# Masked attention on gathered rows: the first batch by its least key, counts and mask sums in the score banks, and transfers in smaller portions

## The chip, the cores and the metric

The kernel runs on one core of one Trainium2 chip. The metric is the device time of one execution in microseconds (us). Before the change the median of three runs is 963.98 us (963.57 to 964.73). The engines have short names in what follows: PE is TensorE (PEld its weight loads, which overlap the matmuls), DVE is VectorE, ACT is ScalarE, POOL is GpSimd, SP is SyncE, which here issues most DMAs. Lines such as L823 are line numbers of the kernel before, unless it is said that they are of the kernel after.

## The reference

There are 16 batches of 512 features by 1024 tokens, fp32, and one mask value (0 or 1) per token and batch. With `xt` the transposed x, per batch:

```python
q = xt @ Wq.T                                   # T x 512, used as q, k and v; 8 heads of 64
scores = scale * einsum('bhqd,bhkd->bhqk', qh, qh)
logits = (scores * cmask + (1.0 - cmask) * NEG) * rmask
attn = softmax(logits, axis=-1)
ctx = einsum('bhqk,bhkd->bhqd', attn, qh)
out = ctx @ Wo.T
return x + transpose(out)                       # residual
```

A masked key gets weight 0. A masked query has all logits 0, so its output is a mean over all tokens, the same row for every masked token of a batch. Only the active tokens (mask 1) need real attention.

## The kernel before, in words

**Only active rows.** At the start the kernel counts the active tokens of each batch with matmuls on the mask, and forms for each batch a key, 32 times the count plus the batch's number (`order`, L198 to L210). The batches are worked in the order of rising keys. For that, DVE ranks all keys against each other: a compare of 16 x 16 pairs and a sum. From then on "batch b" means the batch at place b. `permute` picks the mask of the batch at a place out of all masks, `sources` the number of that batch, from which the base of its rows in memory follows. `slots_of` (one batch, L286 to L316) and `slots` (a group of batches, L244) give each active token its slot, with a prefix count by matmuls against a triangle of ones. `hot` (L356) forms a one-hot matrix of the low part of the slots (128 x 1024 fp16, L360); `index` (L363) multiplies it with a second one-hot matrix on PE (L369) and so gets the list of row numbers (L372). With it `gather` (posted to POOL, indirect DMA, L458) brings the active rows of x from memory, in blocks of 128 rows: four blocks, and a fifth where a batch is handled at 528 or 544 columns instead of 512. At the end the rows of the output are written through the same lists (L1051).

**One batch.** The rows are transposed on PE (`xt`, L562), split into fp16 high and low parts (L520, L521), and multiplied with Wq, also split (`query`, three matmuls a part, L591). Queries are split again and spread by SP into `xx`, a layout in SBUF with both heads of a pair (`qsplit`, L606 to L628). Four pairs of heads follow: `scores` (L823) forms the scores of a pair in two steps, four score tiles each, and ACT takes their exponentials out of PSUM (L838). `attend` (L858) multiplies them with the values. The reciprocals of the sums are formed in two parts: `recip_sums` (DVE, up to L905) and `recip_rows` (L907): a transpose on PE (L912), a copy of ten rows out of PSUM (`rr`, L917), a DMA to DRAM (`rd`, L920) and two DMAs back, which spread the rows over partitions (`rb`, L924). `norm` scales the context with them and splits it (L964 to L968); `project` (L982) multiplies with Wo, and L988 adds the residual.

**PSUM.** In the steady part the tile `pss` has six of the eight banks. Scores use its banks 0 to 4 or a part of them, the context banks 4 and 5; small products ("spots") stand in the first columns of bank 5: the index lists, the score bounds (`top`, `bottom`, L714 to L730). The two banks that are left are a ring, `pm`, which queries, transposes, values, projections, the counts of `slots`, the mask sum (`facts_end`, L351) and most of the reciprocal rows take turn by turn. Waits between writers and readers of one bank are found by the framework from the tiles; where the code knows that two operations touch other parts, it says so (`other_banks`), and where it knows that they touch the same, it adds the wait by hand (`needs`).

**The order of the work.** The order of PE's instructions is written out by hand: each batch has 18 stages. A table `plan` names for each stage, in two halves, what PE does beside scores and context: transposes and queries of the next batch, projections of the batch before, counts of batches ahead. Lists named `free` hold work that begins at a stage. For the other engines a list scheduler of the framework orders the instructions by their priority and by what they need. Counts are formed for groups of places: 0 and 1 one by one, then 2 to 3, 4 to 7, 8 to 10, 11 to 13, 14 to 15.

**The opening.** Before the stages, `run` orders the work in lists: order of the batches, list and gathers of batch 0, splits of Wq, and "warm" matmuls, which compute nothing that is used (L408), while PE has no input. Then come transposes, queries and values of batch 0, the list of batch 1 (`index1`), four of batch 1's five gathers, and a first shift for the exponentials. Loads of Wo (four of 256 KB on SP) and the loads of whole x batches (`load_all`) for the masked tokens' mean are held back until that shift (`first_top`).

In `scores`, the first matmul of a step waits for all four exponentials of the step before (`self.left`):

```python
if n == 0 and self.left:
    self.needs(m.ins, *self.left)
```

Of the kernel before, what the change touches and what calls it, by code (L numbers as in the profile page):

```python
# [10 lines left out]
F32 = mybir.dt.float32  # L11
# [8 lines left out]
P = 128  # L20
D = 512
T = 1024
# [25 lines left out]
class Fast:  # L48
# [12 lines left out]
    def __init__(self, ctx, tc, x, x_nat, mask_t, wq_t, wo_t, out):  # L61
# [13 lines left out]
        self.context_out, self.left, self.read, self.spots, self.spot_reads = None, [], [], False, []  # L75
# [20 lines left out]
    def setup(self, mask_t):  # L96
# [45 lines left out]
        self.rank = fixed("rank", [P, B])  # L142
        self.base = fixed("base", [P, B])
# [54 lines left out]
    def order(self):  # L198
# [7 lines left out]
        key = self.sb([P, B], F32, "sc", 3)  # L206
        nc.vector.scalar_tensor_tensor(key, pn, 32.0, self.number, ALU.mult, ALU.add)
        more = self.sb([P, B, B], F16, "c", 4)
# [35 lines left out]
    def slots(self, b0, b1):  # L244
# [8 lines left out]
        pr = self.pm([P, B, TB])  # L253
        nc.tensor.matmul(pr, lhsT=self.tri, rhs=mh, start=True, stop=False)
        for s in range(1, TB):
            nc.tensor.matmul(pr[:, :, s:], lhsT=self.on16, rhs=mh[:, :, :TB - s], start=False, stop=(s == TB - 1))
        pn = self.pm([P, B])
        for j in range(TB):
            self.pe = nc.tensor.matmul(pn, lhsT=self.on16, rhs=mh[:, :, j], start=(j == 0), stop=(j == TB - 1)).ins
        nc.vector.tensor_copy(n, pn)  # L260
        base = self.sb([P, B, TB], F32, "sc", 3)
        nc.vector.tensor_tensor(base, self.tok.unsqueeze(1).broadcast_to([P, B, TB]), pr, ALU.subtract)
        nc.vector.tensor_tensor(base, base, n.unsqueeze(2).broadcast_to([P, B, TB]), ALU.add)
        slot = self.sb([P, NC], F32, "sc", 3)
        s3 = slot.rearrange("p (b j) -> p b j", j=TB)
        nc.vector.tensor_tensor(s3, pr, base, ALU.subtract)
# [19 lines left out]
    def slots_of(self, b):  # L286
# [5 lines left out]
        whole, half = self.sb([P, 7, TB], F32, "c", 4), self.sb([P, TB, 2 * NB], F16, "c", 4)  # L292
        free, sign, put, base, slot, hi, far = (whole[:, k] for k in range(7))
# [12 lines left out]
        nc.vector.scalar_tensor_tensor(base, free, n, put, ALU.mult, ALU.add)  # L306
        nc.vector.tensor_tensor(slot, sign, pr, ALU.mult)
# [5 lines left out]
        nc.vector.scalar_tensor_tensor(self.lo[:, b], hi, -float(P), far, ALU.mult, ALU.add)  # L313
        nc.vector.tensor_tensor(oh, hi.unsqueeze(2).broadcast_to([P, TB, NB]),
                                self.ionb.unsqueeze(1).broadcast_to([P, TB, NB]), ALU.is_equal)
        nc.vector.tensor_tensor(self.oht[:, b], oh, self.tok.unsqueeze(2).broadcast_to([P, TB, NB]), ALU.mult)  # L316
# [28 lines left out]
    def facts_end(self, b0, b1):  # L345
        nc = self.nc
        B = b1 - b0
        ok = self.ok[:, b0:b1]
        t = self.sb([P, B], F32, "sc", 3)
        pe = self.pm([P, B])  # L350
        nc.tensor.matmul(pe, lhsT=self.on16, rhs=self.whole_masks, start=True, stop=True)  # L351
        nc.vector.tensor_scalar(t, pe, float(T), None, ALU.is_equal)
        nc.vector.tensor_tensor(ok, ok, t, ALU.mult)
# [9 lines left out]
    def index(self, b):  # L363
# [8 lines left out]
        i = s["at"] = nc.vector.tensor_scalar(s["idx"], pi, base, None, ALU.add).ins  # L372
        self.spot_reads += [i] * self.spots
# [40 lines left out]
    def spotted(self, i):  # L414
        if self.spots:
            self.other_banks(i.ins, *self.left)
        return i

# [291 lines left out]
    def top(self, b, g):  # L710
# [5 lines left out]
        with self.tc.high_priority(offset=HPO):  # L716
            i = nc.vector.tensor_reduce(m, pt, AX.X, ALU.max).ins
        if self.spots:
            self.other_banks(i, *self.left)
            self.spot_reads.append(i)  # L720

    def bottom(self, b, g):
# [6 lines left out]
        with self.tc.high_priority(offset=HPO):  # L729
            self.spot_reads += [nc.vector.tensor_scalar(nm[:, :HG], pb, -SCALE, None, ALU.mult).ins] * self.spots  # L730
# [57 lines left out]
    def scores(self, b, p, u):  # L788
# [28 lines left out]
        opening = b == 0 and p == 0 and u == 0  # L817
        if opening:
            calls.sort(key=lambda c: c[0] // (2 * A))
        banks = [c[0] // 512 for c in calls]  # L820
        for n, (c0, c1, w, x) in enumerate(calls):
# [7 lines left out]
            if n == 0 and self.left:  # L829
                self.needs(m.ins, *self.left)  # L830
            last = [m.ins]
        self.beat = last[0]
        self.left, self.context_out = [], None
        ps = {}
        for j in (0, 1, 2, 3) if opening else (3, 0, 1, 2):
# [3 lines left out]
                                     scale=SCALE, accum_out=s["z"][:, 2 * p + k, i:i + 1]).ins  # L839
            self.exp = [e]  # L840
            self.left.append(e)
            ps[k, i] = t
        s.setdefault("p", {}).setdefault(p, {}).update(ps)

    def attend(self, b, p, after=None):
# [7 lines left out]
        for g in (1, 0):  # L853
            cols = slice(g * CH, (g + 1) * CH)
            for i in range(3, -1, -1):
                for k in (1, 0):
# [3 lines left out]
                    self.other_banks(mm.ins, *exps[1 - g:])  # L860
                    if g == 0 and i == 3:
# [3 lines left out]
        self.spot_reads = []  # L865
# [41 lines left out]
    def recip_rows(self, b, p):  # L907
# [8 lines left out]
        with self.tc.high_priority(offset=HPO):  # L916
            self.recip = nc.vector.tensor_copy(rr, pt[:10]).ins  # L917
            self.spot_reads += [self.recip] * spot
# [175 lines left out]
    def run(self, flag):  # L1094
# [52 lines left out]
        with self.tc.high_priority(offset=HPO):  # L1147
            self.order()
            self.permute(0, 1)
            self.active(0, 1)  # L1150
            self.sources(0, 2)
            self.slots_of(0)
            self.hot(0)
        self.warm(6)
# [3 lines left out]
        self.warm(5)  # L1158
        with self.behind(self.st[0]["at"], self.pe):
            with self.tc.high_priority(offset=HPO):  # L1160
                self.permute(1, 2)
                self.active(1, 2)
                self.slots_of(1)
            for f in halves:
                f()
            with self.tc.high_priority(offset=HPO):
                self.sources(2, B)
            self.setup2()
        self.warm(13)
        for i in range(DC):  # L1170
            self.load_half(0, i)
        for k in range(3):
# [3 lines left out]
            if k == 2:  # L1176
                for i in range(DC, 2 * DC):
                    self.load_half(0, i, self.pe)
        def index1():
            with self.behind(self.last_xs):  # L1180
                self.hot(1)
                self.index(1)

# [310 lines left out]
```

## Time and profile before

| what | value |
|---|---|
| median of 3 runs | 963.98 us (963.57 to 964.73) |
| profiled execution, its own time | 965.21 us |
| span of the profile | 963.5 us |
| PE busy | 931.5 us, 97% |
| DVE busy | 721.1 us, 75% |
| ACT busy | 644.7 us, 67% |
| POOL busy | 305.1 us, 32% |
| mean granted clock of PE | 0.999 |

The profile is of one execution. Its span is the time from the first to the last instruction. "Busy" is time in which an engine executes; the chain is followed back from the last instruction, at each step to what released it. In a timeline a row gives start, duration, engine, line and operation, the tile written and the tiles read, the count, and in brackets the idle time before it with what ended that. In a table by stretches a row gives the stretch, its length, busy time of PE, PEld, DVE, ACT and POOL (instructions in brackets), the granted clock of PE, the busy share of the DMA engines (1 is all of the time) and GB/s. In the view of waits, a row names the waiting engine, tile and line, what it waited for, the total in us, how often, and the longest.

### The profile page before, as it was taken

How to read it: one execution, taken by the hardware profiler on the slowest of the kernel's cores; microseconds unless marked ns; L12 is line 12 of the kernel's file. 1: busy time of each engine (PE TensorE's matmuls, PEld its weight loads, DVE VectorE, ACT ScalarE, POOL GpSimd, SP SyncE). 2: the span in 40 equal slices, each digit the busy share in tenths (PEclk: the TensorE clock that was granted, in tenths of full speed). 3: DMA queues.
4: the chain of work that ended last, by engine and by line, in shares of the span. 5: the costliest groups of instructions: out<-in, count | busy, mean ns of one | idle time of the engine just before them, and what ended most of it. 6: DMA issues, size and time to landing. Idle time of an engine off the chain costs nothing.

```text
span 963.5 us, 22790 instructions
## 1 busy us (share of the span) xinstructions
PE 931.5 (97%) x8121; PEld 581.3 (60%) x8121; DVE 721.1 (75%) x2443; ACT 644.7 (67%) x1669; POOL 305.1 (32%) x311
## 2 busy tenths in 40 slices
PE   6799999999999999999999999999999999999997
PEld 4556656566666666666666566666666666565543
DVE  7779677776777767887678687877877788685563
ACT  4778766667677666776767678665767866665651
POOL 2102022142241513415144250522515135252452
PEclk9999999999999999999999999999999999999999
DMA  5756556556675666756656787654767757555552
GB/s 172 222 175 203 155 154 183 163 180 190 180 209 148 194 197 193 220 157 199 177 181 204 198 239 223 177 158 136 214 168 233 243 144 207 151 161 161 171 175 102
DMA packets 78568, 176.30 MB, mean 183 GB/s; under 512 B 14480, under 2 KB 22416, under 8 KB 78448
## 3 DMA queue, kind: packets, MB, share of 16 engines
q1 hardware_dynamic: 57392, 107.09, 39.8%
q0 software_dynamic: 21056, 67.68, 22.4%
q8 instruction: 66, 1.08, 0.5%
q14 instruction: 54, 0.44, 0.2%
HBM read 91.36 MB, written 33.91 MB: 130 GB/s over the span
## 4 chain that ended last, share of the span: by engine, by line
PE 81%; DVE 10%; ACT 4%; DMA 2%; issue 2%; SPq 1%; POOL 0%; POOLq 0%; DVEq 0%; ACTq 0%
PE pss L858 22%; PE pss L823 17%; PE pm L982 17%; PE pm L591 16%; ACT p L838 2%; PE pss L876 2%; PE pm L562 2%; DMA xx<-hl 1%; PE pss L766 1%; PE pm L654 1%; DVE xl L521 1%; PE pss L982 1%; DVE xa L988 1%; PE pm L912 1%; DVE p L777 1%
## 5 line engine op out<-in xcount | busy, mean ns | idle before, releaser
L838 ACT ACTIVATE p<-pss,nm 128x528 f32<-128x528 f32 (+2 forms) x512 | 353.9, 702 | 104.7 <-PE pss L823 101.5
L858 PE MATMUL pss<-p,v 128*64 128x264 f32 (+2 forms) x2048 | 242.4, 389 | 0.0
L823 PE MATMUL pss<-xx 128*128 128x118 f16 (+17 forms) x1856 | 213.6, 287 | 3.9 <-ACT p L838 2.8
L1051 POOL DMA_INDIRECT y_out<-xa,idx x68 | 82.0, 1206 | 405.2 <-DVE nq L732 85.1
L858 PEld LDWEIGHTS pss<-p,v 128*64 128x64 f32 x2048 | 141.4, 137 | 85.8 <-issue 4.9
L823 PEld LDWEIGHTS <-xx 128*128 128x128 f16 (+1 forms) x1856 | 103.2, 96 | 85.1 <-issue 34.3
L591 PE MATMUL pm<-xh,wqh 128*128 128x264 f16 (+5 forms) x512 | 141.8, 277 | 3.3 <-DVE xl L521 1.3
L591 PE MATMUL pm<-xh,wql 128*128 128x264 f16 (+5 forms) x512 | 141.1, 275 | 0.0
L591 PE MATMUL pm<-xl,wqh 128*128 128x264 f16 (+5 forms) x512 | 140.9, 275 | 0.0
L591 PEld LDWEIGHTS <-wqh 128*128 128x128 f16 x1024 | 96.4, 97 | 31.6 <-issue 12.6
L458 POOL DMA_INDIRECT xa<-x_in,idx x68 | 72.5, 1066 | 123.4 <-DMA y_out<-xa,idx 49.1
L838 ACT ACTIVATION_READ_ACCUMULATOR p<-pss,nm 128x1 f32 x512 | 105.2, 205 | 0.0
L982 PE MATMUL pm<-woh,ch 128*128 128x512 f16 x240 | 91.1, 380 | 0.0
L982 PE MATMUL pm<-woh,cl 128*128 128x512 f16 x240 | 90.9, 379 | 0.0
L982 PE MATMUL pm<-wol,ch 128*128 128x512 f16 x240 | 90.9, 379 | 0.0
L595 ACT ACTIVATE q<-pm 128x264 f32<-128x264 f32 (+5 forms) x128 | 50.8, 397 | 43.1 <-PE pm L591 42.7
L988 DVE SCALAR_TENSOR_TENSOR xa<-pm,xa 128x512 f32<-128x512 f32 x61 | 41.6, 681 | 46.0 <-PE pm L982 45.7
L1051 POOL DMA_INDIRECT y_out<-xi,idx x60 | 64.9, 1081 | 33.9 <-PE pss L766 13.4
L658 ACT COPY v<-pm 128x512 f32<-128x512 f32 x64 | 37.5, 586 | 56.0 <-PE pm L654 54.3
L982 PEld LDWEIGHTS <-ch 128*128 128x128 f16 x480 | 44.9, 98 | 47.5 <-issue 4.1
L458 POOL DMA_INDIRECT xi<-x_in,idx x60 | 59.4, 990 | 21.6 <-issue 15.8
L881 ACT COPY c<-pss 128x528 f32<-128x528 f32 (+2 forms) x64 | 38.3, 598 | 37.9 <-PE pss L876 26.8
(249 smaller groups left out, 1485.0 us busy)
## 6 DMA issues: line engine op xcount, KB each, us to landing
xm<-x_nat_in SPq DMA_DIRECT2D x60, 512.0 KB
xx<-hl SPq DMA_DIRECT2D x208, 136.0 KB
rb<-rd SPq DMA_DIRECT2D x72, 132.0 KB
xx<-hl SPq DMA_DIRECT2D x48, 128.0 KB
pt<-c SPq DMA_DIRECT2D x36, 132.0 KB
pt<-p SPq DMA_DIRECT2D x36, 132.0 KB
rb<-rd SPq DMA_DIRECT2D x32, 136.0 KB
ub<-ud SPq DMA_DIRECT2D x16, 256.0 KB
```

What stands on the lines that cost most here:

```text
L458: dma = self.nc.gpsimd.indirect_dma_start(out=tile[:n], out_offset=None, in_=self.x, in_offset=bass.IndirectOffsetOnAxis(ap=idx, axis=0))
L562: self.pe = nc.tensor.transpose(pt[:, c, :], x[:n, c * P:(c + 1) * P], self.ident[:n, :n]).ins
L591: self.beat = nc.tensor.matmul(pq, lhsT=w[:, c, e * P:(e + 1) * P], rhs=xx[:, c, cols], start=(k == 0), stop=(k == 3 * DC - 1)).ins
L595: nc.scalar.activation(s["q"][:, e, cols], pq, AF.Copy, scale=1.0 / (SX * SW))
L658: nc.scalar.copy(v, pv)
L823: m = nc.tensor.matmul(flat[:, c0:c1], lhsT=w, rhs=x, start=banks[n] not in banks[:n], stop=banks[n] not in banks[n + 1:])
L838: e = nc.scalar.activation(t, flat[:, at:at + A], AF.Exp, bias=s["nm"][p // 2][:, p % 2 * 2 + k:p % 2 * 2 + k + 1], scale=SCALE, accum_out ...
L858: mm = nc.tensor.matmul(pav[k * DK:(k + 1) * DK, g], lhsT=s["v"][p][:, i, k * DK:(k + 1) * DK], rhs=ps[k, i][:, cols], start=(i == 3), sto ...
L881: self.context_out = nc.scalar.copy(c[:, :A].rearrange("p (g c) -> p g c", g=2), pav).ins
L982: mm = nc.tensor.matmul(po[:cols.stop - cols.start], lhsT=a[:, e, cols], rhs=w[:, e, :], start=(e == 0 and k == 0), stop=(e == DC - 1 and ...
L988: return self.nc.vector.scalar_tensor_tensor(x, po, 1.0 / (SX * SW), x, ALU.mult, ALU.add).ins
L1051: dma = self.nc.gpsimd.indirect_dma_start(out=self.out, out_offset=bass.IndirectOffsetOnAxis(ap=idx, axis=0), in_=x, in_offset=None)
```

## The change

- The first batch is found by the least key: a minimum over the 16 keys, and its mask as the sum over batches of (key equals the minimum) times mask. Ranking all keys is a function of its own (`ranks`), called after the splits of Wq are listed. Base and first row of batch 0 come from its count and the least key.
- The one-hot matrix, one DVE operation of 128 x 1024, becomes eight operations of 128 x 128 inside `slots_of`.
- The warm matmuls before the first rows: 6, index, 5, counts of batch 1, 13 become 5, index, 13. Source and counts of batch 1 stand behind the fourth transposes of batch 0, its list behind the second group's query 1. Its gathers come in two parts: two blocks behind query 2 of batch 0, three in stage 0 of batch 0. In batch 0's plan the transposes of the next batch are divided 4 and 1 among the two halves of stage 5 (before 3 and 2).
- In `scores` of batch 0, each bank's first matmul waits for the exponential of its own bank only, and the exponentials for their own bank's matmuls, in the order in which the banks are complete. In `attend` of batches with 512 columns the context no longer waits for exponentials that read other banks.
- The counts (`slots`) and the mask sums (`facts_end`) are written to bank 5 of `pss` instead of the ring; `slots` goes from stage 6 to the second half of stage 7, behind query 1 (in batch 0 from 9 to 8). The mask sum of batches 0 and 1 goes from the opening to stage 3.
- The reciprocal rows of pair 1 go from the start of stage 10 to the end of the first half of stage 10 (in batch 0 of stage 11).
- Wo is loaded at stages 3, 6, 9 and 12 of batch 0, one quarter each, behind the scores matmul issued last (`beat`), instead of all at stage 2; the loads of whole batches in batch 0 are held back by `beat` too.

```diff
@@ order, ranks
+        nc.vector.tensor_reduce(self.least, key, AX.X, ALU.min)
+        each = self.sb([P, TB, B], F16, "hl", 2)
+        nc.vector.scalar_tensor_tensor(each, key.unsqueeze(1).broadcast_to([P, TB, B]), self.least,
+                                       mh.rearrange("p b j -> p j b"), ALU.is_equal, ALU.mult)
+            nc.vector.tensor_reduce(self.act16[:, 0], each, AX.X, ALU.add)
+
+    def ranks(self):
+        nc, B, key = self.nc, self.B, self.key
         more = self.sb([P, B, B], F16, "c", 4)
...
@@ slots
-        pr = self.pm([P, B, TB])
-        nc.tensor.matmul(pr, lhsT=self.tri, rhs=mh, start=True, stop=False)
+        spot = self.spot(NC + B)
+        pr, pn = spot[:, :NC].rearrange("p (b j) -> p b j", j=TB), spot[:, NC:]
+        self.spotted(nc.tensor.matmul(pr, lhsT=self.tri, rhs=mh, start=True, stop=False))
...
-        pn = self.pm([P, B])
...
+        with self.tc.high_priority(offset=HPO):
+            reads = [nc.vector.tensor_copy(n, pn),
...
+        self.seen(*(reads[k] for k in (0, 1, 3)))
@@ slots_of
+        if b == 0:
+            who = self.base[:, 0:1]
+            nc.vector.scalar_tensor_tensor(who, n, -32.0, self.least, ALU.mult, ALU.add)
+            nc.vector.tensor_copy(self.first_row[:, 0:1], who[0:1, :])
+            nc.vector.tensor_scalar(who, who, float(T), None, ALU.mult)
...
+        ol = self.st[b]["ol"] = self.sb([P, TB, P], F16, "tmp", 2)
...
-        nc.vector.tensor_tensor(self.oht[:, b], oh, self.tok.unsqueeze(2).broadcast_to([P, TB, NB]), ALU.mult)
+        for j in range(TB):
+            nc.vector.tensor_scalar(ol[:, j], self.io128, lo[:, j:j + 1], None, ALU.is_equal)
+            if j == 2:
+                nc.vector.tensor_tensor(self.oht[:, b], oh, self.tok.unsqueeze(2).broadcast_to([P, TB, NB]), ALU.mult)
@@ facts_end
-        pe = self.pm([P, B])
-        nc.tensor.matmul(pe, lhsT=self.on16, rhs=self.whole_masks, start=True, stop=True)
-        nc.vector.tensor_scalar(t, pe, float(T), None, ALU.is_equal)
+        pe = self.spot(B)
+        self.spotted(nc.tensor.matmul(pe, lhsT=self.on16, rhs=self.whole_masks, start=True, stop=True))
+        with self.tc.high_priority(offset=HPO):
+            self.seen(nc.vector.tensor_scalar(t, pe, float(T), None, ALU.is_equal))
@@ new
+    def seen(self, *reads, free=True):
+        if self.spots:
+            for i in reads:
+                self.other_banks(i.ins, *self.left)
+                self.spot_reads.append(i.ins)
+                self.free_reads += [i.ins] * free
@@ scores
-            if n == 0 and self.left:
+            if alone and self.left:
+                own = (1, 2, 3, 0)[banks[n]]
+                if banks[n] not in banks[:n]:
+                    self.needs(m.ins, self.left[own])
+                self.other_banks(m.ins, *(e for k, e in enumerate(self.left) if k != own))
+            elif n == 0 and self.left:
                 self.needs(m.ins, *self.left)
...
+            if alone:
+                self.other_banks(e, *(m for m, bank in zip(mms, banks) if bank != j))
@@ attend
-                    self.other_banks(mm.ins, *exps[1 - g:])
-                    if g == 0 and i == 3:
+                    self.other_banks(mm.ins, *exps[(1 - g) * (self.reach > 512):])
+                    if g == 0 and i == 3 and self.reach > 512:
                         self.needs(mm.ins, *exps[:1])
@@ run, the opening
             self.order()
-            self.permute(0, 1)
-            self.active(0, 1)
-            self.sources(0, 2)
             self.slots_of(0)
-            self.hot(0)
-        self.warm(6)
+        self.warm(5)
         self.index(0)
         for j in range(4):
             self.gather(0, j)
-        self.warm(5)
+        self.warm(13)
...
-        first = query(0, 0, 0) + xt(0)[3:] + [(0, L(self.facts, 0, 2))] + query(0, 1, 0) + query(0, 0, 1)
+        first = query(0, 0, 0) + xt(0)[3:] + [(0, slots1)] + query(0, 1, 0) + query(0, 0, 1)
...
-        first += [(0, index1)] + sums0[:4] + value(0, 0) + g1[:1] + query(0, 1, 1)[:1] + g1[1:2]
-        first += value(0, 1) + split1 + sums0[4:] + query(0, 2, 0) + g1[2:3] + query(0, 2, 1)[:1] + g1[3:4]
+        first += sums0[:4] + value(0, 0) + query(0, 1, 1)[:1] + [(0, index1)]
+        first += value(0, 1) + split1 + sums0[4:] + query(0, 2, 0) + g1[:2] + query(0, 2, 1)[:1]
+        first += [(0, L(self.sources, 2, B))]
@@ run, the stages (batches 1 to 14)
-                                (5, 1): vt(b, 1) + pk(b, 1), (6, 0): post,
-                                (7, 0): third + q(1, 0) + tp(b, 1), (7, 1): q(1, 1) + P_(0) + bt(b, 1), (8, 0): tc(0) + v(0) + end + rng[:2],
-                                (10, 0): tv(0) + tail + q(2, 0), (11, 0): hot + rng[2:] + early,
+                                (5, 1): vt(b, 1) + pk(b, 1),
+                                (7, 0): third + q(1, 0) + tp(b, 1), (7, 1): q(1, 1) + post + P_(0) + bt(b, 1), (8, 0): tc(0) + v(0) + end + rng[:2],
+                                (10, 0): tv(0) + tail + q(2, 0) + turn, (11, 0): hot + rng[2:] + early,
@@ run, Wo and whole batches
-                        free.setdefault(2, []).append(L(self.load, "o", c, None, first_top))
+                        free.setdefault(3 * c + 3, []).append(lambda c=c: self.load("o", c, None, self.beat))
...
-                        free.setdefault(at, []).append(L(self.load_all, x, c, None if b else first_top))
+                        free.setdefault(at, []).append(L(self.load_all, x, c) if b else lambda x=x, c=c: self.load_all(x, c, self.beat))
```

91 lines of the change are left out of this document (49 added, 42 removed).

## The prediction, made before the change was run

> **What bounds the kernel now.** I read the page first (busy shares, chain), then busy time by stretches, then what TensorE waited for, opening and rest apart.
>
> ```profile
> span 963.5 us, 22790 instructions
> PE 931.5 (97%) x8121; PEld 581.3 (60%) x8121; DVE 721.1 (75%) x2443; ACT 644.7 (67%) x1669; POOL 305.1 (32%) x311
> PE 81%; DVE 10%; ACT 4%; DMA 2%; issue 2%; SPq 1%; POOL 0%; POOLq 0%; DVEq 0%; ACTq 0%
> 0.00:10.00 10.00, 3.56 (x31) 1.67 (x32) 6.50 (x28) 4.39 (x9) 2.98 (x30) 1.00 0.51 147
> 30.00:40.00 10.00, 6.84 (x44) 3.52 (x44) 6.94 (x25) 6.23 (x20) 2.59 (x3) 1.00 1.03 277
> 80.00:90.00 10.00, 8.96 (x95) 5.79 (x94) 9.94 (x38) 8.18 (x24) 1.90 (x2) 1.00 0.74 239
> ```
>
> TensorE is the bound: 97% busy, 81% of the chain. Its work hardly changes, so only its idle time can go: 963.5 − 931.5 = 32 us. The first 10 us hold 6.4 of it; 30 to 40 us hold 3.2, with the DMA engines saturated (share 1.03); around 80 to 90 us VectorE is 99% busy and sets the pace. The profiled execution took 965.21, 1.7 outside the span; that is 1.2 above the median of the runs, 963.98.
>
> The waits of TensorE, first 0 to 60 us, then the rest (total, times, longest):
>
> ```profile
> PE pm L205 <- DVE given L202: 3.9, 1, 3.9
> PE pm L300 <- DVE act L227: 2.3, 1, 2.3
> PE pss L823 <- ACT p L838: 2.3, 2, 1.8
> PE pm L651 <- ACT q L595: 1.2, 3, 0.6
> PE pm L912 <- DVE xl L521: 1.1, 1, 1.1
> PE pm L351 <- DVE eh L342: 0.5, 1, 0.5
> ```
>
> ```profile
> PE pm L912 <- DVE rcol L905: 2.3, 3, 1.2
> PE pm L351 <- DVE xa L988: 2.1, 5, 0.4
> PE pm L254 <- DVE tmp L683: 1.6, 4, 0.4
> PE pm L591 <- DVE rr L917: 1.1, 7, 0.2
> PE pm L982 <- DVE rr L917: 0.6, 4, 0.2
> PE pm L912 <- DVE n L260: 0.3, 1, 0.3
> ```
>
> The edits aim at most of these rows. The prices follow by part of the span.
>
> **A. Start, up to batch 0's first rows.** The order of events on VectorE, TensorE and GpSimd:
>
> ```profile
> 4.46 0.17 DVE L207 SCALAR_TENSOR_TENSOR sc<-pm,number 128x16 f32<-128x16 f32 x1 [0.58 <-PE pm L205]
> 4.67 0.42 DVE L209 TENSOR_TENSOR c<-sc 128x256 f16<-128x256 f32 x1
> 6.29 0.29 DVE L227 TENSOR_REDUCE act<-hl 128x8 f16<-128x128 f16 x1
> 8.58 1.22 DVE L360 TENSOR_TENSOR tmp<-io,lo 128x1024 f16<-128x1024 f16 x1
> 9.71 0.23 DVE L316 TENSOR_TENSOR oht<-c,tok 128x72 f16<-128x72 f16 x1
> 10.62 0.28 DVE L384 TENSOR_SCALAR hr<-row,n 128x128 f32<-128x128 f32 x1
> 10.81 0.38 DVE L224 TENSOR_TENSOR hl<-c,given 128x128 f16<-128x128 f16 x1
> 26.49 0.29 DVE L616 COPY hl<-hl 128x512 f16<-128x512 f16 x1
> 10.21 2.29 PE L408 MATMUL warm<-on 128*128 128x512 f16 x5
> 12.75 2.97 PE L408 MATMUL warm<-on 128*128 128x512 f16 x13
> 10.91 1.30 POOL L458 DMA_INDIRECT xa<-x_in,idx  x1 [7.11 <-DVE hr L384]
> 15.55 0.60 PE L562 MATMUL pss<-ident,xa 128*128 128x128 f32 x4
> ```
>
> Ranking: from key (4.46) to the row of active tokens (6.29) are 1.83 us, over seven further operations. After the change it is a minimum (0.17 as L207), a compare-times-mask (0.38, L224's) and a sum (L227's 0.29), 0.84: −1.0.
>
> One-hot: L360 to L316 is 1.13 us. Eight pieces of 128 columns replace it. Bounds for one: 0.19 (the spacing for which L384's tensor_scalar, fp32, held VectorE, 10.62 to the next start at 10.81), 8 × 0.19 = 1.5, a loss of 0.4; and 0.07, a quarter of L616's 0.29 for 512 fp16 columns, 0.6, a gain of 0.5. I take 0.10: the pieces are fp16 from SBUF as L616 is, and L616's time hardly exceeds that of L384's 128 columns, so most of it is a latency that back-to-back operations overlap. −0.3. The index matmuls start under the pieces, −0.2.
>
> [...]
>
> So row numbers come 1.5 earlier (0.8 to 1.7); the four gathers (first at 10.91) move with them, and the first transposes of x rows (15.55). Thirteen warm matmuls now run straight after the index matmuls, and the 16 count matmuls for batch 1 (L300 to L304) leave their place ahead of them. Those counts now stand in the query stage: 0.25 of TensorE (between the end of the five at 12.50 and the thirteen at 12.75) and as much of waiting, against the removed L351 row (0.5): zero. The L651 waits (1.2) lose part of their cover, because index(1) and batch 1's gathers leave that stretch: +0.3. The ranking, run later, falls on VectorE behind wq's splits, where TensorE waits for rows from memory; hidden. If it weren't, it costs the 1.0. **A = −1.3** (−0.5 to −2.0).
>
> A clock rule bears on the warm matmuls: five together took 2.29 (0.43 apiece with latency), thirteen 2.97 (0.22 apiece), though the granted clock stands at 1.00 in the windows. [...]
>
> **B. 31 to 60 us, batch 0's first scores.**
>
> ```profile
> 28.73 0.60 SPq L628 DMA_DIRECT2D xx<-hl  x1
> 33.25 1.13 PE L823 MATMUL pss<-xx 128*128 128x512 f16 x4 [1.03 <-DMA xx<-hl]
> 38.02 1.36 PE L823 MATMUL pss<-xx 128*128 128x512 f16 x6 [1.78 <-ACT p L838]
> 43.24 1.04 PE L823 MATMUL pss<-xx 128*128 128x512 f16 x4 [0.50 <-ACT p L838]
> 51.46 0.33 PE L912 MATMUL pm<-ident,rcol 128*128 128x128 f32 x1 [1.07 <-DVE xl L521]
> 75.59 2.67 DMA xx<-hl
> ```
>
> Scores waited 1.03 for a spread issued at 28.73 and used at 33.25 (4.5 us), where a later one (75.59, from the chain) took 2.67. Out of that stretch go four loads of Wo, now one each at stages 3, 6, 9 and 12, and three of five gathers of batch 1, now in stage 0, so GpSimd's queue is empty sooner. I take the 1.0 as gone (0 to −1.0); the loads themselves have 10 stages before they are used, nothing waits. In batch 0, scores now wait per bank for the exponential that read that bank, and exponentials for their own bank's matmuls: the 1.78 and the 0.50 go, −2.3, unless the exponentials, back to back, are the pace there. The context matmul may also start before all exponentials (no price: it was covered by transposes). The 1.07 at L912 is a wait for a buffer of the PSUM ring; twelve transposes instead of eight stand there, and the third now needs the split of the first: the same 1.1 comes back, plus 0.6 of other ring waits from denser work. **B = −2.7** (0 to −3.5).
>
> **C. 60 to 110 us.** VectorE is 99% busy at 80 to 90. What TensorE gains before it may have to wait off here. The added VectorE work, the moved sums of masks and counts, is of 0.17 us operations. I take +0.4 (−0.6, half of the longest wait at L905, to +1.2, that wait doubled).
>
> **D. The other 14 batches.** The reciprocal rows of pair 1 go from ahead of a matmul group to the end of a stage's fill: the eleven waits on rr go, 1.1 + 0.6 = −1.7; nothing reads their result for eight stages. In their new place the copy still holds a ring buffer, but the next taker is a stage away; next late is the spread to all partitions. Counts leave the ring for bank 5: 1.6 + 0.3 = −1.9; the price is a read that must precede the next writers of that bank, under the scores' exponentials, hidden. The waits at L905 (2.3) stay. For the sum of masks (L351) I expect no gain:
>
> ```profile
> 110.57 0.15 DVE L730 TENSOR_SCALAR nm<-pss 128x4 f32<-128x4 f32 x1
> 110.70 0.16 PE L351 MATMUL pm<-eh,on 128*128 128x2 f16 x1 [0.41 <-DVE xa L988]
> ```
>
> It now writes the bank that L730 reads, and L730's read ends at 110.72, 0.02 after the start of before; with a handover of 0.05 each of the five starts 0.07 later. So 2.1 stays, and +0.4. **D = −3.2** (−0.5 to −3.6).
>
> **Sum:** −1.3 − 2.7 + 0.4 − 3.2 = −6.8. The profiled execution becomes 958.4, the median 957.2. A measurement tells 0.2% from no change: faster is below 962.05, slower above 965.91.
>
> **The rivals.**
>
> *R1, VectorE takes the start's gain back.* Around 80 to 90 us VectorE sets when TensorE goes on. If it gets through no earlier, for its work is the same, A and B (−4.0) are lost there and D stays, and C's +0.4: 963.98 − 3.2 + 0.4 = 961.2. For it: 9.94 of 10 busy. Against: VectorE isn't full at 30 to 40 (6.94) and work may start earlier there.
>
> *R2, ring waits move.* The waits of D reappear at the next taker of the PSUM ring, for VectorE's list is the same. Then A to C remain, −3.6: 960.4. Against: the counts take no ring buffer at all afterwards.
>
> *R3, the clock.* The thirteen warm matmuls now begin near 8.7, some 4 us earlier; at 0.22 to 0.43 apiece they end at 11.7 to 14.3, and the first transposes stand near 14. If TensorE falls back to the slow pace in that gap and runs 6 us of early matmuls at 0.43 where 0.22 would do, that is +3 and the sum −3.8: 960.2. For it: the two warm rows. Against: the gap is 0 to 2 us, and earlier gaps are shorter than before. [...]
>
> *R4, the other side.*
>
> ```profile
> 257.58 0.32 SPq L920 DMA_DIRECT2D rd<-rr  x1
> 259.28 1.12 SPq L924 DMA_DIRECT2D rb<-rd  x2
> ```
>
> SyncE issues in order, and between rd and rb it stands 1.4 us (257.90 to 259.28) for rd to land. Moved to the end of stage 10's fill, which batches 0 to 14 have, this pair stands ahead of the spreads of the next batch's query parts, which scores and tail work wait for. If their slack of several stages is used up, each of 15 batches pays up to 1.4 plus the 1.12 of rb's issue; at 0.7 it is +10.5: 963.98 − 6.8 + 10.5 = 967.7. It decides from 0.58 a batch ((6.8 + 1.93)/15). Against: the view of waits after 60 us has no row on xx.
>
> *No change*: each removed wait is replaced on the spot, 963.9.
>
> **Chances.** Forecast 0.58 (its own range 955.3, with the low ends of A, B and D, to 960.1, with half of B and D); R1 0.15, a quarter of it within 0.2%; R2 0.09, a fifth of it within; R3 0.06; R4 0.10; no change 0.02. Faster 0.58 + 0.11 + 0.07 + 0.06 = 0.82; same 0.04 + 0.02 + 0.02 = 0.08; slower 0.10. The range runs over the forecast and R1 to R3, from 954.3, the own range with C's low end, to 962.0; it leaves out R4, no change and the high ends taken together.
>
> **What would show it.** Right: the first gather near 9.4 and first query matmul near 16; eight pieces under 1 us in all; no L823 wait of more than 0.5 on an exponential in batch 0; DMA share below 1 at 30 to 40; no waits on rr, none at L254; mask-sum waits still there. Wrong: a new wait for xx or rb in every batch (R4), the same time of the first scores of batch 1 as before (R1), new ring waits at L591 or L982 (R2), 0.4 us matmuls at 17 to 25 us (R3).

## The result, and the profile after

The changed kernel takes 959.87 us (median of 6 runs, 958.53 to 960.91), the kernel before 963.89 (6 runs): a ratio of 0.9951, with a 95% interval of 0.9939 to 0.9962. The forecast was 957.2 with a range of 954.3 to 962.0. Direction and range hold; two terms of the sum do not, and their errors have opposite signs, so that the range was met in part by luck.

The profiled execution took 959.46 with a span of 957.8, 5.7 less than the span before. Of that, 1.0 us is not the change's: VectorE's first operation on the masks (`given`, L203; L202 before) started 0.2 earlier and took 0.23 instead of 1.06. It takes 1.06 to 1.14 in five of the fourteen traces of this case and 0.23 to 0.25 in the nine others, and the kernel with all mends has one of each; why is open. That leaves 4.7, which is nearer to the 4.0 by medians. Line numbers from here on are those of the kernel after, unless it is said otherwise.

What TensorE waited for in the changed kernel, up to 60 us (the two rows that the forecast speaks of) and after it (total, times, longest):

```profile
PE pm L682 <- ACT q L626: 1.8, 3, 1.0
PE pm L593 <- DVE xl L552: 1.6, 1, 1.6
```

```profile
PE pss L745 <- DVE smcol L739: 2.6, 1, 2.6
PE pss L373 <- DVE nm L758: 2.5, 5, 0.5
PE pm L952 <- ACT q L626: 1.9, 4, 0.5
PE pm L952 <- DVE rcol L945: 1.3, 2, 1.1
PE pm L685 <- DMA xx<-hl: 1.2, 1, 1.2
PE pm L622 <- DVE xl L552: 0.5, 2, 0.3
PE pm L622 <- DVE rr L957: 0.4, 1, 0.4
```

The waits on exponentials (but for 0.2 in batch 15), on `rr` (all but one) and at the triangle matmul are gone. The five waits of the mask sum (L373) stay, as forecast. New are a wait of 2.6 at the score bound (L745), one of 1.2 for a spread (L685), and four of 0.5 ahead of the reciprocal rows (L952).

Where the gain stands can be followed on the exponentials, which both kernels take in the same order. Here are the first of the third step of batch 0 and the first of the third step of batch 1, before:

```profile
44.92 0.69 ACT L838 ACTIVATE p<-pss,nm 128x512 f32<-128x512 f32 x1 [1.26 <-PE pss L823]
97.97 0.71 ACT L838 ACTIVATE p<-pss,nm 128x544 f32<-128x544 f32 x1 [0.23 <-PE pss L823]
```

and after:

```profile
39.76 0.69 ACT L873 ACTIVATE p<-pss,nm 128x512 f32<-128x512 f32 x1 [0.66 <-PE pss L851]
97.83 0.71 ACT L873 ACTIVATE p<-pss,nm 128x544 f32<-128x544 f32 x1 [0.24 <-PE pss L851]
```

The changed kernel is 5.2 us ahead in batch 0 and 0.1 ahead in batch 1. All that the opening had won was gone between these two places, and what is left at the end, 5.7, was won again by the batches behind. The stretch where it is lost, in busy time by stretches and in the order of events on SyncE, ScalarE, VectorE and TensorE:

```profile
70.00:80.00 10.00, 6.18 (x50) 3.50 (x47) 6.29 (x20) 6.30 (x18) 2.26 (x2) 0.96 1.01 302
80.00:90.00 10.00, 10.00 (x97) 6.81 (x95) 8.77 (x30) 6.25 (x17) 1.82 (x2) 0.87 0.61 173
```

```profile
69.65 0.37 SPq L541 DMA_DIRECT2D xm<-x_nat_in  x1
74.94 1.06 ACT L526 ACTIVATE xm<-xm 128x1024 f32<-128x1024 f32 x1 [3.15 <-DMA xm<-x_nat_in]
76.46 0.59 ACT L689 COPY v<-pm 128x512 f32<-128x512 f32 x1
77.08 0.69 DVE L672 TENSOR_TENSOR tmp<-v 128x512 f32<-128x512 f32 x1 [2.83 <-ACT v L689]
79.04 0.30 PE L745 MATMUL pss<-ident,smcol 128*128 128x128 f32 x1 [2.65 <-DVE smcol L739]
75.07 0.28 PE L622 MATMUL pm<-xh,wql 128*128 128x272 f16 x1
79.81 0.43 PE L622 MATMUL pm<-xh,wqh 128*128 128x274 f16 x1
```

The row at 75.07 stands there for comparison. Read from the top: the seventh load of a whole-batch part is issued at 69.65 and lands after 5 us, with the DMA engines saturated (1.01). ScalarE stands 3.15 in the sum over it (L526). Behind that sum in ScalarE's order is the copy of the values (L689); VectorE needs it for the squares; from the squares comes the score bound; TensorE waits 2.65 for that. Then its matmuls take 0.43 instead of 0.28, for the granted clock is down (0.96 and 0.87 in the two stretches: 0.4 + 1.3 us lost). With the 1.2 that TensorE waits for a spread at 72.97 that makes 5.5; the kernel before has waits of 1.4 of its own in that stretch, which are gone.

### The profile page after: what moved, and what is told of

The parts are those of the page before. It is cut to its first block, busy times and chain, and to the rows that moved or that the text cites. A ratio compares the mean times of both kernels' runs of the same rounds, so it can differ in the third digit from the quotient of the medians.

```text
span 957.8 us, 22828 instructions
## 1 busy us (share of the span) xinstructions
PE 930.3 (97%) x8115; PEld 581.8 (61%) x8115; DVE 719.6 (75%) x2460; ACT 644.3 (67%) x1669; POOL 305.3 (32%) x311
## 4 chain that ended last, share of the span: by engine, by line
PE 83%; DVE 8%; ACT 4%; DMA 3%; issue 1%; SPq 0%; POOL 0%; POOLq 0%; DVEq 0%; ACTq 0%
PE pss L898 22%; PE pss L851 17%; PE pm L1023 17%; PE pm L622 16%; PE pss L916 2%; ACT p L873 2%; PE pm L593 2%; PE pss L794 1%; DVE xl L552 1%; PE pm L685 1%; DMA xm<-x_nat_in 1%; PE pss L1023 1%; PE pm L952 1%; DMA xx<-hl 1%; DVE p L805 1%
## 5 line engine op out<-in xcount | busy, mean ns | idle before, releaser
L1092 POOL DMA_INDIRECT y_out<-xa,idx x68 | 79.1, 1163 | 410.0 <-DVE nq L760 113.7
L689 ACT COPY v<-pm 128x512 f32<-128x512 f32 x64 | 37.5, 586 | 58.7 <-PE pm L685 56.0
```

The costliest lines, as they stand in the source:

```text
L689: nc.scalar.copy(v, pv)
L1092: dma = self.nc.gpsimd.indirect_dma_start(out=self.out, out_offset=bass.IndirectOffsetOnAxis(ap=idx, axis=0), in_=x, in_offset=None)
```

## The experiments

In the first set (the four kernels up to "exponentials wait for all banks") the kernel before takes 964.49. In the second and third the same kernel takes 983 and 979 (the last run: 983), for reasons outside the kernels; from those sets I use the ratios within a set, the traces up to 110 us, and the kinds of waits, not absolute times.

One number serves for most of them, called the loss: by how much the lead over the kernel before, in the starts of exponentials shown above, shrinks between the third step of batch 0 (44.92 before) and the third step of batch 1 (97.97). For the changed kernel it is 5.16 − 0.14 = 5.0.

**Loads of whole batches held back as before.** Theory L: the order of the loads.

```diff
-  free.setdefault(at, []).append(L(self.load_all, x, c) if b else lambda x=x, c=c: self.load_all(x, c, self.beat))
+  free.setdefault(at, []).append(L(self.load_all, x, c, None if b else first_top))
```

> Loads of whole batches held back by the shift (first_top) as before the change; the rest as changed. Theory L (order of loads): in the changed kernel the seventh whole-batch load is issued at 69.65, behind four spreads; ScalarE waits 3.15 for it in its sum (L526), TensorE then 2.65 at the score bound (L745) and 1.17 at a value product, and runs at half clock for 3.4 us. With this edit that load stands ahead of the spreads in SyncE's order: the waits go, the first scores of batch 1 come 4 to 5 us earlier, time 955 to 956. Theory W (the staged Wo loads crowd the DMA engines there): no change, 959.9. Theory V (VectorE gives the start's gain back whatever is loaded, rival R1): other waits take the place, 959 to 960.

Measured: 960.09 (957.3 to 968.4, 12 runs), ratio 0.996 (0.994 to 0.9981). The loss is 5.7. ScalarE's wait at that place is gone, and VectorE stands in its place: it waits 2.9 for the eighth load, with the score bound behind that sum. The order is what made the seventh load late: it is issued at 62.1 here instead of 69.65. With it in time the eighth takes its place (issued at 73.85), so the 4 to 5 us of Theory L do not come. TensorE also waits 2.6 in all for spreads here, and its clock is halved for 3.4 us: late transfers reach it directly too, not through the sums alone.

**Wo at stage 2 as before.** Theory W: the staged loads of Wo crowd the DMA engines.

```diff
-  free.setdefault(3 * c + 3, []).append(lambda c=c: self.load("o", c, None, self.beat))
+  free.setdefault(2, []).append(L(self.load, "o", c, None, first_top))
```

> All four loads of Wo at stage 2 as before the change; the rest as changed. Theory L: the seventh whole-batch load still stands behind the spreads, so the wait of ScalarE at 70 to 75 us stays; the crowd at 30 to 40 us comes back and costs up to 1.0 there, which the wait swallows: 959.5 to 960.5. Theory W: the wait goes, 955 to 956. Theory V: 959 to 960, with no wait on a whole-batch load.

Measured: 959.65, ratio 0.9956 (0.994 to 0.9972). A wait of 2.2 at L745 stays, the loss is 2.9. Theory W falls too. The staged Wo is worth nothing that these runs show.

**Both loads as before.**

```diff
-  free.setdefault(3 * c + 3, []).append(lambda c=c: self.load("o", c, None, self.beat))
+  free.setdefault(2, []).append(L(self.load, "o", c, None, first_top))
...
-  free.setdefault(at, []).append(L(self.load_all, x, c) if b else lambda x=x, c=c: self.load_all(x, c, self.beat))
+  free.setdefault(at, []).append(L(self.load_all, x, c, None if b else first_top))
```

> Wo at stage 2 and whole-batch loads behind the shift, as before the change; the rest as changed. Theory L: the seventh load is ahead of the spreads, so the large wait goes; the four Wo loads at 30 to 40 us cost 0 to 1.0: 955 to 957. Theory W: 955 to 957 too. Theory V: 959 to 960.

Measured: 957.82, ratio 0.9933 (0.9917 to 0.9949): better than the changed kernel by the ratios, though the intervals overlap. A wait of 2.5 at the second product of the score bound stays, behind VectorE's wait of 2.9 for the eighth load; the clock does not fall in this execution. The loss is 1.8.

**Exponentials wait for all banks again.**

```diff
-        alone = b == 0
+        alone = False
...
-        done = sorted(range(4), key=lambda j: len(banks) - banks[::-1].index(j)) if alone else (3, 0, 1, 2)
+        done = (0, 1, 2, 3) if b == 0 and p == 0 and u == 0 else (3, 0, 1, 2)
```

> Scores of batch 0 wait for all four exponentials again, exponentials for all matmuls of their step; the rest as changed. If the prediction's step B is right, the waits of 1.8 and 0.5 on L838 of before come back (some 2.3 by 45 us into the span). At the end: by theory L the wait at 70 to 75 us hangs on a load in SyncE's queue, not on TensorE, and swallows most of it: 959.5 to 960.5; without such a swallow 962.

Measured: 961.27, ratio 0.9966 (0.9953 to 0.9978). The two waits come back to the tenth:

```profile
35.53 1.57 PE L851 MATMUL pss<-xx 128*128 128x512 f16 x8 [1.79 <-ACT p L873]
40.75 1.57 PE L851 MATMUL pss<-xx 128*128 128x512 f16 x8 [0.50 <-ACT p L873]
```

so this part of step B is right in mechanism and size (2.3). At the end 1.4 us by the medians are left of it, though the intervals of the ratios overlap.

**Theory T.** What all four share are late whole-batch loads with sums in the order of an engine that has something urgent behind the sum. Theory T says that these sums are the mechanism. Its rival is VectorE's own work (rival R1 of the prediction, "V" in the expectations).

**Most whole-batch loads left out.** Each whole batch of batch 0's stages loads only its first quarter, whose tile stands for the others; the other three quarters are left out, and the sums over them read the first one again.

```diff
-  free.setdefault(at, []).append(L(self.load_all, x, c) if b else lambda x=x, c=c: self.load_all(x, c, self.beat))
+  free.setdefault(at, []).append(L(self.load_all, x, c) if b else (lambda x=x, c=c: self.load_all(x, c, self.beat)) if c == 0 else lambda x=x: self.st[x]["xm"].append(self.st[x]["xm"][0]))
```

> In batch 0 only the first quarter of each of the two whole batches is loaded (1 MB instead of 4 MB); its sum stands in for the other quarters, so the rows of masked tokens are wrong for two batches. The rest as changed. Theory T (the whole-batch loads set the pace at 60 to 85 us: the eighth lands at 77 to 80 in every variant so far, and the sums on ScalarE or VectorE stand in front of the score bound): no wait of more than 0.5 at the score bound, the gain of 45 us lives on to batch 1 (-4 to -5 against before at its first scores instead of -0.7), 955.5 to 956.5. Theory V (VectorE's own work is the pace there): waits on VectorE of 2 us in all stay without any load, 959 or more.

Measured: ratio 0.9949 (0.9928 to 0.997), in the second set. The loss is 0.0 (a lead of 4.0 at both places). The waits from 60 to 110 us:

```profile
PE pss L745 <- DVE smcol L739: 0.5, 1, 0.5
PE pss L373 <- DVE nm L758: 0.5, 1, 0.5
PE pm L622 <- ACT v L689: 0.4, 1, 0.4
PE pm L622 <- DVE xl L552: 0.2, 1, 0.2
```

VectorE does the same sums here; it only need not wait for their data. So its own work does not take the lead back, and R1 as I had put it falls. The run also takes the traffic of these loads away (the wait for a spread is gone too), so by itself it does not tell late sums from full DMA engines.

**Whole-batch loads and sums three stages earlier.**

```diff
-                        at = 3 * c + k + (0 if b else 4)
+                        at = 3 * c + k + (0 if b else 1)
```

> The whole-batch loads of batch 0 and their sums three stages earlier (stages 1 to 11 instead of 4 to 14); the rest as changed. Theory T: the eighth load is issued ahead of the spreads and gathers of 65 to 77 us, the wait at the score bound falls below 1 us; against it stands more traffic at 34 to 45 us, up to 1.0: 955.5 to 957.5. If the sum of bytes rather than their order were the limit, the wait would come back elsewhere: 959 to 960.

Measured: ratio 1.0038 (1.0013 to 1.0064). The sums now stand too early:

```profile
PE pm L593 <- DVE xl L552: 6.2, 1, 6.2
```

The same mechanism 30 us earlier (at 48.6): VectorE waits 4.1 for a load, and the split that TensorE's transposes need is queued behind the sum. ScalarE stands 3.6 in such a sum just before, ahead of exponentials, and so at 44.92 of before this kernel has no lead at all.

**Counts back in the ring** (two runs of one kernel).

```diff
-        spot = self.spot(NC + B)
-        pr, pn = spot[:, :NC].rearrange("p (b j) -> p b j", j=TB), spot[:, NC:]
+        pr = self.pm([P, B, TB])
...
+        pn = self.pm([P, B])
...
-  (5, 1): vt(b, 1) + pk(b, 1),
+  (5, 1): vt(b, 1) + pk(b, 1), (6, 0): post,
...
-  (7, 1): q(1, 1) + post + P_(0) + bt(b, 1)
+  (7, 1): q(1, 1) + P_(0) + bt(b, 1)
```

> Counts of the groups back in the ring of PSUM tiles and at stage 6 (in batch 0 at stage 8); the rest as changed. By the prediction's step D the stalls of 0.4 at the triangle matmul come back in batches 2, 6, 9 and 12: 4 x 0.41 + 0.25 = +1.9. The trace of the changed kernel gained more there, -0.7, -1.4, -1.1 and -0.9 between scores 1 and 5 of these batches and -1.4 at the end of batch 2; if all of that is due to the counts, +4 to +5.5, 964 to 965.

> The kernel of counts_in_ring once more (counts of the groups in the ring and at stage 6, the rest as changed), since the earlier run stood among times of 983 for the kernel before, which leave a difference of 2 us open. By the prediction's step D +1.9 against the changed kernel, 961.8; by the offsets in the changed kernel's trace up to +5, 964 to 965.

Measured: ratios 1.0013 (0.9985 to 1.0041) and 0.9982 (0.9958 to 1.0006), in the second and third set; against the changed kernel's 0.9951 that is +3 to +6 us, though of other sets. The stalls come back exactly where they were, in batches 2, 6, 9 and 12; the view of waits behind 110 us in the second of the runs, with the line numbers of its own kernel:

```profile
PE pm L265 <- DVE tmp L712: 1.6, 4, 0.4
```

The loss of these two is 3.1 and 2.1: with untouched loads and sums it varies, from 2.1 to 5.0 over the executions seen.

**Reciprocal rows of pair 1 as before.**

```diff
-                            if p != 1 or n == B:
-                                free.setdefault(st + 2, []).append(L(self.recip_rows, b, p))
+                            free.setdefault(st + 2, []).append(L(self.recip_rows, b, p))
...
-  turn = [(0.1, L(self.recip_rows, b, 1))]
+  turn = []
```

> The reciprocal rows of pair 1 at the start of stage 10 again; the rest as changed. By the prediction's step D, +1.7. By the trace of the changed kernel the move gave -0.31 in eight batches and cost +0.39 in five (2, 5, 8, 11, 14), where a projection's tail stands in the same fill: together -0.5, so 960.0 to 960.8.

Measured: ratio 0.9962 (0.9937 to 0.9987), in the second set, not to be told from 0.9951. The waits on `rr` are back behind 110 us, and the row of L952 waiting for ScalarE's copy of q is gone:

```profile
PE pm L622 <- DVE rr L957: 1.2, 8, 0.2
PE pm L1023 <- DVE rr L957: 0.6, 4, 0.2
```

So the move exchanged one ring wait for another.

**The last two sums later.** Theory T in its narrow form: loads and bytes untouched, only the seventh and eighth sum moved.

```diff
-  free.setdefault(at + (2 if b + 2 in self.extra else 4), []).append(...)
+  free.setdefault(17 if b == 0 and c == 3 else at + (2 if b + 2 in self.extra else 4), []).append(...)
```

> The sums over the last whole-batch loads of batch 0 (the seventh and eighth) stand at stage 17 instead of 15 and 16, so in ScalarE's order the seventh sum comes behind the next context copy, value copy, four exponentials and a query, and in VectorE's the eighth behind the score bound of batch 1; loads and all else as changed. Theory T in its narrow form (not the bytes but the place of the sums in the engines' order makes TensorE wait for late loads): the wait of 2.6 at the score bound and the half clock behind it go, the first scores of batch 1 come 3 to 4.5 us earlier than in the changed kernel, 955.5 to 957. If the DMA engines themselves (busy share 1.01 at 70 to 80) set the pace, another wait on a transfer takes its place, 959 to 960.

Measured: ratio 0.9945 (0.9922 to 0.9967), in the third set. The loss falls to 0.8. On ScalarE the copy of the values no longer stands behind a load, and the sum waits for nothing:

```profile
74.63 0.59 ACT L921 COPY c<-pss 128x512 f32<-128x512 f32 x1 [1.97 <-PE pm L952]
75.11 0.59 ACT L689 COPY v<-pm 128x512 f32<-128x512 f32 x1
79.04 1.09 ACT L526 ACTIVATE xm<-xm 128x1024 f32<-128x1024 f32 x1
```

The wait at L745 is 1.1, and the clock stays at 1.00 from 70 to 90 us. The bytes of these loads are the same, so by these rows it is the place of the sum in the engine's order that lets a late load reach TensorE. Two things weaken this. The ninth load, which needs the seventh's buffer, now goes out at 82.9 instead of 76.1, and the DMA engines are less full from 70 to 80 (0.87 instead of 1.01). And in the same set the kernel with the counts in the ring, its sums untouched, has a wait of 1.1 at the score bound as well, with a loss of 2.1; the comparison within the set is thus 2.1 against 0.8, of one trace each. The whole time shows less than the expected 3 to 4.5: 0.9945 cannot be told from the changed kernel's 0.9951.

**All mended** (two runs of one kernel): the sums later, both loads as before, the mask sum ahead of a projection part, and the reciprocal rows of pair 1 at stage 12 where a projection's tail stands in stage 10.

```diff
...
-  (5, 1): vt(b, 1) + pk(b, 1),
+  (5, 1): vt(b, 1) + pk(b, 1), (6, 0): masks,
...
-  (7, 1): q(1, 1) + post + P_(0) + bt(b, 1), (8, 0): tc(0) + v(0) + end + rng[:2],
+  (7, 1): q(1, 1) + post + end + P_(0) + bt(b, 1), (8, 0): tc(0) + v(0) + rng[:2],
-  (10, 0): tv(0) + tail + q(2, 0) + turn,
+  (10, 0): tv(0) + tail + q(2, 0) + ([] if tail else turn),
-  (12, 0): q(2, 1),
+  (12, 0): (turn if tail else []) + q(2, 1),
...
```

> Sums later as in last_sums_later, loads of Wo and of whole batches issued as before the change, the sum of masks ahead of the projection part at stage 7 instead of behind the score bound's second product (its DVE part at stage 6), and the reciprocal rows of pair 1 at stage 12 ahead of query 2 where a projection's tail stands in stage 10. Against the changed kernel: -3 to -4.5 from the sums, -2.1 to -2.5 from five mask-sum waits of 0.5, -1.5 from five ring waits at L952 and their batches: 952 to 955. If theory T falls, 955 to 957.

> The kernel of all_mended once more, since its first run stood among times of 979 for the kernel before, and its ratio there (0.9855) holds the part of the mends that matters only where transfers and instructions come late. If the kernel before takes 964 here, the list of mends gives 952 to 955, a ratio of 0.988 to 0.991, with no half-clock stretch between 20 us and the end; if the first ratio was the mends' own, 950.

Measured: ratios 0.9855 (0.9823 to 0.9888) and 0.9895 (0.9861 to 0.9929) to the kernel before of the same set. It beats both kernels; in the third set it also took 964.76 beside 973.78 of the kernel with the later sums alone. The loss is 0.2 and 0.3. Its waits from 60 to 110 us in the first run:

```profile
PE pm L622 <- DVE xl L552: 0.8, 1, 0.8
PE pss L745 <- DVE smcol L739: 0.5, 1, 0.5
```

The five mask-sum waits (2.5) are one of 0.8, the four at L952 on q are gone. The absolute 952 to 955 could not be tested, since no set had the kernel before at 964 again.

## Why the prediction was right, and where not

**A (−1.3).** Right in sum, though the terms as listed (−1.0, −0.3, −0.2 and +0.3) add up to −1.2. The pieces of the start, after:

```profile
3.43 0.17 DVE L208 SCALAR_TENSOR_TENSOR key<-pm,number 128x16 f32<-128x16 f32 x1 [0.58 <-PE pm L206]
4.33 0.29 DVE L215 TENSOR_REDUCE act<-hl 128x8 f16<-128x128 f16 x1
6.62 0.57 DVE L336 TENSOR_SCALAR tmp<-io,c 128x128 f16<-128x128 f16 x3
7.25 0.90 DVE L336 TENSOR_SCALAR tmp<-io,c 128x128 f16<-128x128 f16 x5
8.96 1.13 POOL L489 DMA_INDIRECT xa<-x_in,idx  x1 [5.16 <-DVE idx L395]
15.73 0.27 PE L622 MATMUL pm<-xh,wqh 128*128 128x256 f16 x1 [0.25 <-ACT xh L551]
```

From key to the row of active tokens 0.90 instead of 1.83: −0.93, forecast −1.0. The one-hot pieces were mis-sized: five span 0.90 with a last one of 0.25 (their median), so they follow each other at 0.16, 1.3 in all, against my 0.10 and against 1.13 for the one operation; the sign "under 1 us in all" did not come. That is a loss of 0.2 where I had taken a gain of 0.3. The index matmuls under the pieces give the 0.2 back. Key to first gather went from 10.91 − 4.46 = 6.45 to 8.96 − 3.43 = 5.53: −0.9, at the short end of 0.8 to 1.7. The first query matmul came 2.0 earlier, 1.0 of it the quicker operation on the masks.

**B (−2.7).** Right: the lead grew from 2.0 at the first query matmul to 5.2 at the third step of batch 0, and stood at 4.25 at 59.22 of before. The 1.03, 1.78 and 0.50 are gone. The ring wait came where I had put it, with 1.6 instead of 1.1, and L682 waits a little more for q (1.8).

**C (+0.4, −0.6 to +1.2).** Wrong, and the step on which the forecast of the size failed. It is +4.1 in the profiled execution (lead 4.25 to 0.14); over the executions with untouched loads the loss from the third step is 2.1 to 5.0. I had looked at VectorE's busy share there (9.94 of 10) and asked whether its work would hold TensorE; I had not asked which of that work waits for a transfer. In the kernel before neither of the last two sums waits for more than 0.1 (the issues of their loads are the first two rows):

```profile
64.84 0.34 SPq L510 DMA_DIRECT2D xm<-x_nat_in  x1
72.20 0.43 SPq L510 DMA_DIRECT2D xm<-x_nat_in  x1
75.18 1.07 ACT L495 ACTIVATE xm<-xm 128x1024 f32<-128x1024 f32 x1
76.84 1.22 DVE L502 TENSOR_REDUCE ms<-xm 128x1 f32<-128x1024 f32 x1
```

By the trace's record of landings the seventh load had landed at 69.15, 6.0 ahead of its sum. A lead of 4 alone would not have used that up: the changed kernel also issues this load behind four spreads, 4.8 later than before (69.65), and it lands at 74.92. The eighth had no such room. It landed at 76.82 before and lands at 79.90 after, so work that comes 4 us earlier finds it missing. R1's outcome (the lead is lost by 90 us) thus came by another mechanism than R1's. Leaving out the loads (loss 0.0) and, with the loads kept, moving the sums (0.8) point to it, with the limits said there. What fixes the landing time of the eighth load itself was not settled: it needs a free one of two buffers, SyncE's turn, and DMA engines that are saturated there (share 1.01 from 70 to 80).

**D (−3.2).** The sum came out at −5.6, with errors in both directions. The mask sum is exact: 2.5 instead of 2.1 (its handover of 0.05 stands in the trace of before, where L988 on VectorE ended at 110.65 and L351 started at 110.70). The waits on `rr` went, but what was late next was the ring: in the five batches with a projection's tail ahead of it (2, 5, 8, 11 and 14; the 1.9 at L952 are four of them) each lost 0.3 to 0.4, and the other nine gained 0.3 or less: −0.4 in place of −1.7. I had said that the next taker of the ring was a stage away and had not looked at who held the tiles ahead. The four batches with counts gained 3.9 between their first and fifth steps, where I had 1.9: 1.6 are the stalls, 1.4 two waits that I had not connected with the change (0.69 on a split in batch 6, 0.69 on a gather in batch 9), the rest smaller gaps beside the stalls. A wait of 1.2 at the reciprocal rows in batch 2 went too. In the traces of the runs with the counts back in the ring these three did not come back, so they do not hang on the counts; which edit removed them is open.

**The rivals.** R2 happened in part (L952). R3 did not happen at its place: the first query matmuls took 0.27. Its mechanism did happen at 79 us: behind the pause of 2.65, matmuls took 0.43 instead of 0.28. R4 did not happen: the only wait on `xx` is the 1.2 of the crowded stretch.

**Sum.** −5.7 in the profiled execution against −6.8; by medians −4.0. The kernel before was profiled 1.3 above its median of 963.89, the kernel after 0.4 below, which makes the 1.7 between the two; 1.0 of it is the operation on the masks. C came out 3.7 worse than forecast and D 2.4 better: the two errors largely cancel, and without the second the time would stand at 962.3, just outside the range. That it stayed inside is in part luck.

## What to carry to other kernels

A gain ahead of a stretch is kept only if everything that the stretch waits for comes earlier too: for each transfer used there, compare the landing with the first use, and take the difference as the most that the lead can be before it is eaten; and see that the change does not issue the transfer later. An operation that reads a transfer nobody needs soon belongs behind the urgent work in its engine's order. Moving two such sums took the loss to 0.8, holding both loads as before to 1.8, in one trace each; the ratios of the two do not tell which is worth more. When an operation leaves a PSUM ring or moves in it, follow which operation takes the freed turn.

## What the runs showed of the hardware

In these traces, pauses of TensorE shorter than the slow stretch behind them cost clock. In the changed kernel the pause of 2.65 was followed by matmuls of 0.43 instead of 0.28 until 82.6, a stretch of 3.4 us. In the kernel with exponentials waiting for all banks a pause of 1.66 was enough, with one of 0.17 behind it:

```profile
91.32 0.43 PE L593 MATMUL pm<-ident,xt 32*128 32x32 f32 x4 [1.66 <-DVE xl L552]
92.54 0.43 PE L622 MATMUL pm<-xh,wqh 128*128 128x272 f16 x1
90.00:100.00 10.00, 8.52 (x68) 5.80 (x70) 9.44 (x25) 6.46 (x19) 0.00 (x0) 0.83 0.50 137
```

(the third line is the stretch: clock 0.83, so 1.7 us lost), while the 2.5 of the kernel with both loads as before was followed by none, with a clock of 1.00 up to 90.

The clock records of the traces narrow this down. In all fourteen, between the opening and the end, the half-clock stretches begin and end on steps of 3.41 us, counted from where the full clock sets in: in the changed kernel full from 10.96, half at 79.22, twenty steps later, full again at 82.63. In the kernel before the full clock sets in at 12.53, between the two rows of warm matmuls that the prediction compares (0.43 and 0.22 apiece). I took TensorE's idle time in each step at full clock, by its matmul rows. All twelve steps with 1.83 us or more were followed by half clock (2.65 in the changed kernel, 1.83 in the kernel with exponentials waiting for all banks). Of some 3,870 with less, two were (1.73 and 1.27), and the highest that was not had 1.82. The pause of 2.5 with both loads as before fell on two steps, 1.0 in one and 1.6 in the other. In these traces, then, about half a step of idle time costs 1.7 us, and a pause can escape by where it falls. That fits the spread of the changed kernel's runs (958.5 to 960.9), though no run was made to show that it is the cause.

In the second and third set TensorE also stood around 1 us ahead of score matmuls several times (6.9 us in eight, in the kernel with the later sums) for nothing that the profile shows; in the changed kernel's own trace there is no such row. The kernel with all mends had 4.5 in five of them. What they are stays open.
